# A reordered last slice, finer pieces at its end, a finer start and matmuls on an identity in an attention-over-graphs kernel

## The chip, the cores and the metric

One core of one Trainium2 chip. The metric is the time of one execution on the device in microseconds (us), lowest is best. Engines are named as in the profile: PE or TensorE (matmuls), PEld (its weight loads), DVE or VectorE, ACT or ScalarE, POOL or GpSimd, SP (the queue that issues transfers). "The clock" is the clock that TensorE is granted, as a share of full speed.

## The reference

128 graphs of 128 nodes with 768 features. Each is normalised over its features, cut at zero, projected to queries, keys and values (12 heads of 64), and attends within itself under a mask with an additive bias; the result is added to the input.

```python
def reference(x, adj, Wq, bq, Wk, bk, Wv, bv, beta):
    h = maximum(layernorm(x), 0)                      # x: 128 x 128 x 768, seen as 128 graphs
    q, k, v = heads(h @ Wq + bq), heads(h @ Wk + bk), heads(h @ Wv + bv)     # 12 heads of 64
    s = q @ k.T / 8 + beta * adj
    s = where(adj > 0, s, -9e15)
    return x + merge(softmax(s) @ v)
```

## The kernel before

The graphs go through in 32 groups of four (`GRP = 4`). Per group there are three **slices** of the projection: the queries and keys of six heads ("qk0"), the values ("v") and the queries and keys of the other six ("qk1"). Save for the very first slice, which is computed plainly, each slice is computed in 15 **products** of sums of blocks, with corrections that VectorE adds on. While TensorE works through a slice, the attention of three **head pairs** is fed in between its products: `scores` (16 matmuls in the profile's count, then bias on VectorE and exponential on ScalarE) and, four products later, `attend` (16 matmuls, division on VectorE, addition of the residual on GpSimd, store).

```python
    def bias_1(G, raw):                      # the masked bias of a group, from its adjacency
        a = work.tile([P, GRP, N], F32, tag="adjT", name=f"adjT_{G}", bufs=1)
        nc.vector.transpose(a, raw.rearrange("p g b j -> p g (b j)"))
        kp = work.tile([P, GRP, N], U8, tag="kp", name=f"kp_{G}", bufs=1)
        nc.vector.tensor_scalar(kp, a, 0.0, None, op0=ALU.is_gt)
        nc.vector.tensor_scalar(a, a, beta_c, BIAS_CAP * ISCALE, op0=ALU.mult, op1=ALU.min)
        t = biasT[G] = work.tile([P, GRP, N], F32, tag="biasT", name=f"biasT_{G}", bufs=2)
        nc.gpsimd.memset(t, MASKED)
        nc.vector.copy_predicated(t, kp, a)
        nc.scalar.activation(a, a, AF.Square)
        return a

    def bias_2(G, a):                        # its largest square, for the overflow flag
        bm = stat.tile([P, GRP], F32, tag="bm", name=f"bm_{G}", bufs=1)
        nc.vector.tensor_reduce(bm, a, AX.X, ALU.max)
        nc.vector.tensor_tensor(seen_b, seen_b, bm, ALU.max)
    # ... cut
    def attention(G, u):                     # head pairs 3u, 3u+1, 3u+2, among a slice's products
        todo = {}
        for i in range(3):
            todo.setdefault(1 + 4 * i, []).append(lambda oc=3 * u + i: scores(G, oc))
            todo.setdefault(5 + 4 * i, []).insert(0, lambda oc=3 * u + i: attend(G, oc))
        return todo

    def slice_of(G, sl, todo):
        for n in range(len(PRODUCTS)):
            product(G, sl, n)
            for f in todo.get(n, ()):
                f()
    # ... cut
    HB = GRP * NB // 2
    first = {}

    def half(r, step):                       # the first group is normalised in two halves
        lo = r * HB
        if step == 0:
            for g in range(2):
                stats(0, 2 * r + g)
        elif step == 1:
            first[r] = moments_1(0, lo, lo + HB)
        else:
            first["pool"] = moments_2(0, lo, lo + HB, *first[r])   # ends in a power on GpSimd
            for g in range(2):
                norm(0, 2 * r + g)                                 # ScalarE
            for k in range(3):
                first["dve"] = to_hT(0, r, k)                      # transpositions on VectorE
    # ... cut
    def behind_adds(f, *args):               # puts f behind the latest correction on VectorE
        with tc.issue_after(added[0].ins):
            return f(*args)
    # ... cut: in the loop over the groups, the slice qk1 of group 0
        if not G:
            for n in range(8):
                then(n, lambda n=n: behind_adds(sum_weights, "qk0", n))
            then(13, lambda: bias_2(1, bias_1(1, load_adj(1))))
    # ... cut: after the loop, the last three head pairs, with nothing left to lie beside
    last = attention(NG - 1, 1)
    for n in sorted(last):
        for f in last[n]:
            f()
    # ... cut: worst, over, a matmul and "bad", the overflow flag that decides whether a
    #          second, general program has to run
```

## Time and profile before

| | before |
|---|---|
| time, median of 3 | 3136.41 us (3132.30 to 3136.93) |
| the profiled run | 3132.11 us; span 3130.3 us, mean clock 0.997 |
| TensorE busy | 99% of the span |

The prediction shows the busy line, the list of TensorE's waits, the chain of work at the stall and the tail, and the timeline of the stall. Three more pieces are needed, all from the timeline of the kernel before. Columns: start, length in us, engine and line, operation, written tile <- read tiles, shapes, count, and in brackets the idle time of that engine ahead of it with what ended it.

```profile
10.37 1.66 POOL L244 TENSOR_TENSOR rstd<-ve,nhalf 128x8 f32<-128x8 f32 x1
...
16.68 5.89 PE L402 MATMUL plain<-A,qk_T 128*128 128x256 f32 x16 [6.90 <-DVE A L262]
...
71.52 7.12 ACT L255 ACTIVATE x<-x,shift,rstd 128x192 f32<-128x192 f32 x16 [20.01 <-POOL shift L246]
...
78.55 0.61 ACT L288 ACTIVATE adjT<-adjT 128x512 f32<-128x512 f32 x1
...
79.19 0.69 DVE L293 TENSOR_REDUCE bm<-adjT 128x4 f32<-128x512 f32 x1 [2.85 <-ACT adjT L288]
...
3122.97 1.26 POOL L375 TENSOR_TENSOR xo<-xo,o 128x512 f32<-128x512 f32 x1 [5.50 <-DVE seen L373]
...
3123.14 1.11 DVE L519 TENSOR_SCALAR over<-worst 128x2 f32<-128x2 f32 x1
```

The first two lines are the start: a power on GpSimd ahead of the first normalisations, and the first 16 matmuls, which begin after TensorE has idled for 6.9 us. The next three are a chain across engines: ScalarE normalises group 1 (16 pieces), squares group 0's bias behind them, and VectorE sits 2.85 us waiting for that square. The last two are the end: the comparison for the flag runs at the same time as the last residual addition on GpSimd, and takes 1.11 us for 2 columns.

### The profile page before, as it was taken

How to read it: one execution, taken by the hardware profiler on the slowest of the kernel's cores; microseconds unless marked ns; L12 is line 12 of the kernel's file. 1: busy time of each engine (PE TensorE's matmuls, PEld its weight loads, DVE VectorE, ACT ScalarE, POOL GpSimd, SP SyncE). 2: the span in 40 equal slices, each digit the busy share in tenths (PEclk: the TensorE clock that was granted, in tenths of full speed). 3: DMA queues.
4: the chain of work that ended last, by engine and by line, in shares of the span. 5: the costliest groups of instructions: out<-in, count | busy, mean ns of one | idle time of the engine just before them, and what ended most of it. 6: DMA issues, size and time to landing. Idle time of an engine off the chain costs nothing.

```text
span 3130.3 us, 46295 instructions
## 1 busy us (share of the span) xinstructions
PE 3099.0 (99%) x17822; PEld 2748.1 (88%) x17822; DVE 1999.5 (64%) x5137; ACT 800.6 (26%) x1697; POOL 378.0 (12%) x308
## 2 busy tenths in 40 slices
PE   8999999999999999999999999999999999999998
PEld 7888888888888888888888888888888888888887
DVE  7866566666566665666656666656666566675554
ACT  2222222322222222222222232222222222223221
POOL 1111111111110111111111111111011111111110
PEclk9999999999999999999999999999999999999998
DMA  5212112121122121221211212112211122111111
GB/s 153 70 50 55 43 50 64 51 55 44 45 65 58 48 56 40 57 61 51 55 41 51 65 48 58 44 45 65 57 49 52 44 57 61 51 52 39 49 41 32
DMA packets 358385, 169.94 MB, mean 54 GB/s; under 512 B 84368, under 2 KB 358032, under 8 KB 358160
## 3 DMA queue, kind: packets, MB, share of 16 engines
q1 hardware_dynamic: 355296, 166.14, 19.5%
q8 instruction: 142, 2.33, 0.3%
q10 hardware_dynamic: 2864, 0.79, 0.1%
q14 instruction: 83, 0.68, 0.1%
HBM read 116.53 MB, written 50.33 MB: 53 GB/s over the span
## 4 chain that ended last, share of the span: by engine, by line
PE 98%; DVE 1%; ACT 0%; DMA 0%; issue 0%; POOL 0%; DVEq 0%; ACTq 0%
PE pc_qk L312 18%; PE pb_qk L312 14%; PE pa_qk L312 14%; PE av L364 11%; PE pc_v L312 9%; PE pb_v L312 7%; PE pa_v L312 7%; PE pd_qk L312 7%; PE sc L351 7%; PE pd_v L312 4%; PE plain L402 1%; ACT x L255 0%; DMA x<-in_x_dram 0%; DVE A L262 0%; PE pm L226 0%; PE pm L239 0%
## 5 line engine op out<-in xcount | busy, mean ns | idle before, releaser
L375 POOL TENSOR_TENSOR xo<-xo,o 128x512 f32<-128x512 f32 x192 | 261.1, 1360 | 2455.5 <-DVE seen L373 1539.2
L355 ACT ACTIVATE e<-e 128x512 f32<-128x512 f32 x384 | 235.6, 630 | 780.0 <-DVE e L354 779.3
L364 PEld LDWEIGHTS av<-v,e 128*128 128x128 f32 x3072 | 375.4, 193 | 15.4 <-ACT e L355 5.4
L255 ACT ACTIVATE x<-x,shift,rstd 128x192 f32<-128x192 f32 x512 | 227.9, 533 | 587.4 <-POOL shift L246 587.4
L364 PE MATMUL av<-v,e 128*128 128x65 f32 x3072 | 366.8, 273 | 4.7 <-ACT e L355 4.7
L312 PE MATMUL pb_qk<-S,qk_T 128*128 128x256 f32 x1512 | 367.2, 386 | 0.0
L333 ACT ACTIVATE qk<-pc_qk,bqk 128x256 f32<-128x256 f32 x378 | 158.1, 469 | 726.5 <-PE pc_qk L312 726.5
L354 DVE SCALAR_TENSOR_TENSOR e<-sc,biasT 128x512 f32<-128x512 f32 x384 | 246.8, 685 | 128.2 <-PE sc L351 128.2
L312 PEld LDWEIGHTS pb_qk<-S,qk_T 128*128 128x128 f32 x1512 | 277.3, 190 | 40.2
L337 DVE TENSOR_TENSOR qk<-qk,pb_qk 128x512 f32<-128x512 f32 x252 | 172.1, 683 | 159.4 <-PE pb_qk L312 142.3
L312 PE MATMUL pc_qk<-S,qk_B 128*128 128x256 f32 x1008 | 246.5, 388 | 2.7 <-ACT qk L333 2.7
L312 PE MATMUL pa_qk<-S,qk_T 128*128 128x256 f32 x1008 | 244.7, 386 | 0.0
L312 PE MATMUL pc_qk<-S,qk_T 128*128 128x256 f32 x1008 | 238.1, 379 | 0.0
L351 PE MATMUL sc<-qk 64*128 64x128 f32 x3072 | 224.4, 285 | 0.0
L262 DVE STREAM_TRANSPOSE A<-x 128x256 f32<-128x256 f32 x384 | 217.4, 611 | 8.1 <-ACT x L255 8.0
L312 PEld LDWEIGHTS pc_qk<-S,qk_B 128*128 128x128 f32 x1008 | 187.3, 191 | 33.9 <-ACT qk L333 3.1
L312 PEld LDWEIGHTS pc_qk<-S,qk_T 128*128 128x128 f32 x1008 | 191.5, 190 | 26.0
L351 PEld LDWEIGHTS sc<-qk 64*128 64x128 f32 x3072 | 187.1, 188 | 30.1 <-issue 21.2
L312 PEld LDWEIGHTS pa_qk<-S,qk_T 128*128 128x128 f32 x1008 | 186.3, 190 | 30.4
L312 PE MATMUL pb_v<-v_T,S 128*128 128x256 f32 x768 | 184.2, 382 | 0.0
L337 DVE TENSOR_TENSOR qk<-qk,pd_qk 128x512 f32<-128x512 f32 x126 | 86.6, 688 | 150.0 <-PE pd_qk L312 150.0
L370 DVE TENSOR_TENSOR o<-av,rs 128x256 f32<-128x256 f32 x384 | 160.2, 418 | 2.1 <-DVE seen L373 0.4
(108 smaller groups left out, 4475.1 us busy)
## 6 DMA issues: line engine op xcount, KB each, us to landing
xo<-in_x_dram SPq DMA_DIRECT2D x192, 256.0 KB, 2.8
out_dram<-xo SPq DMA_DIRECT2D x192, 256.0 KB, 2.2
x<-in_x_dram SPq DMA_DIRECT2D x504, 96.0 KB, 2.4
adj<-in_adj_dram SPq DMA_DIRECT2D x128, 64.0 KB, 2.3
qk_T<-in_L_gnn_Wq_dram SPq DMA_DIRECT2D x10, 128.0 KB, 3.4
qk_T<-in_L_gnn_Wk_dram SPq DMA_DIRECT2D x10, 128.0 KB, 3.3
v_T<-in_L_gnn_Wv_dram SPq DMA_DIRECT2D x5, 256.0 KB, 5.5
qk_B<-in_L_gnn_Wq_dram SPq DMA_DIRECT2D x8, 128.0 KB, 3.4
```

The costliest lines, as they stand in the source:

```text
L255: nc.scalar.activation(t, t, AF.Relu, bias=shift[G, n], scale=rstd[G, n])
L262: last = nc.vector.transpose(t[:, :, g * N:(g + 1) * N].rearrange("p c (b i) -> p c b i", i=SQ), src)
L312: nc.tensor.matmul(p[:, i, :], lhs, rhs, start=(first and i == 0 and c == 0), stop=(c == 1), skip_group_check=True)
L333: nc.scalar.activation(t[:, i, :], p[:, i, :], AF.Identity, bias=bqk[:, i, oc:oc + 1], scale=float(sign))
L337: added[G] = nc.vector.tensor_tensor(t, t, p, ALU.add if sign > 0 else ALU.subtract)
L351: nc.tensor.matmul(ps[i][:, g, :], t[r, 1, at], t[r, 0, at], start=True, stop=True)
L354: nc.vector.scalar_tensor_tensor(e, ps[i], SCORE_CAP * ISCALE, biasT[G], op0=ALU.min, op1=ALU.add)
L355: nc.scalar.activation(e, e, AF.Exp, scale=1.0 / ISCALE)
L364: nc.tensor.matmul(pa[:, 2 * g + i, :], es[G, oc, i][:, 2 * r + g, :], vt[G, "v", r, h // 4][:, 4 * g + h % 4, :], start=True, stop=True)
L370: nc.vector.tensor_mul(o[:, r], pa[:, :, 0:HD], rs.to_broadcast([P, 4, HD]))
L375: nc.gpsimd.tensor_add(t, t, o.rearrange("p a (b j) d -> p (a b) (j d)", j=2))
L402: nc.tensor.matmul(p[:, i, :], b[:, c, i * P:(i + 1) * P], a[:, c, :], start=(k == 0 and i == 0 and c == 0), stop=(c == 1), skip_group_che ...
```

## The change

Its intent: (1) the first two graphs are normalised each for itself, so that TensorE's first operand is there earlier; (2) ten matmuls of the identity run in the idle time ahead of it, to bring the clock up; (3) the bias of group 1 is put behind VectorE's corrections in its queue; (4) the last slice's products stand in another order, all six remaining head pairs of the last group are fed in among them, and three of these pairs in halves (two graphs each), with their residual added on VectorE.

```diff
+LAST = (0, 1, 2, 3, 5, 7, 6, 10, 11, 9, 4, 12, 8, 13, 14)
     ... cut: `squares[0]` remembers the second moment matmul; `weigh` is the division taken out of `attend`
+    def scores_half(G, oc, r):               # two graphs: 8 matmuls instead of 16
+        t = xo[G, oc, r] = work.tile([P, 2, P], F32, tag="xo", name=f"xo_{G}_{oc}_{r}", bufs=3)
+        nc.sync.dma_start(t, x[...])
+        ... cut
+    def attend_half(G, oc, r):
+        ... cut
+        weigh(G, oc, r, pa, o)
+        t = xo[G, oc, r]
+        nc.vector.tensor_add(t, t, o.rearrange("p (b j) d -> p b (j d)", j=2))
+        nc.sync.dma_start(out[...], t)
-    def slice_of(G, sl, todo):
-        for n in range(len(PRODUCTS)):
+    def slice_of(G, sl, todo, order=range(len(PRODUCTS))):
+        for at, n in enumerate(order):
             product(G, sl, n)
-            for f in todo.get(n, ()):
+            for f in todo.get(at, ()):
                 f()
-    HB = GRP * NB // 2
+    PARTS = (((0, NB), (NB, 2 * NB)), ((2 * NB, 4 * NB),))
     def half(r, step):
+        for lo, hi in PARTS[r]:
+            ... cut: the same steps, for the graphs of (lo, hi)
+    with tc.issue_after(squares[0].ins):
+        warm = psum.tile([P, P], F32, tag="mm", name="warm")
+        for n in range(10):
+            nc.tensor.matmul(warm, ident, ident, start=True, stop=True)
-            then(13, lambda: bias_2(1, bias_1(1, load_adj(1))))
+            then(13, lambda: bias_2(1, behind_adds(bias_1, 1, load_adj(1))))
-        slice_of(G, "qk1", todo)
-    last = attention(NG - 1, 1)
-    for n in sorted(last):
-        for f in last[n]:
-            f()
+        if G + 1 < NG:
+            slice_of(G, "qk1", todo)
+            continue
+        todo = {}
+        for at, f, *args in (
+            (0, scores, 0), (3, attend, 0), (3, scores, 1), (6, attend, 1), (6, scores, 2), (9, attend, 2),
+            (9, scores_half, 5, 0), (10, scores_half, 4, 0), (11, attend_half, 5, 0), (12, scores_half, 3, 0),
+            (12, attend_half, 4, 0), (13, scores_half, 3, 1), (13, attend_half, 3, 0), (14, scores_half, 5, 1),
+            (14, attend_half, 3, 1), (14, scores_half, 4, 1), (14, attend_half, 5, 1), (14, attend_half, 4, 1),
+        ):
+            then(at, lambda f=f, args=args: f(G, *args))
+        slice_of(G, "qk1", todo, LAST)
```

## The prediction

> **What bounds the kernel now.** I read the page's busy line first, then the list of what the matmul engine waited for over the whole execution, then the chain that ended last in the two places those waits point to.
>
> ```profile
> PE 3099.0 (99%) x17822; PEld 2748.1 (88%) x17822; DVE 1999.5 (64%) x5137; ACT 800.6 (26%) x1697; POOL 378.0 (12%) x308
> ```
>
> ```profile
> PE pm L226 <- DVE st L217: 7.7, 1, 7.7
> PE plain L402 <- DVE A L262: 6.9, 1, 6.9
> PE av L364 <- ACT e L355: 4.7, 3, 1.7
> PE pc_qk L312 <- ACT qk L333: 2.7, 1, 2.7
> PE pf L522 <- DVE over L519: 2.6, 1, 2.6
> PE pm L239 <- DVE dev L233: 0.9, 1, 0.9
> ```
>
> TensorE is busy 3099 of 3130 us, and all its waits are single events: the start (7.7 + 0.9 + 6.9), one stall of 2.7, and the end (4.7 in three pieces, 2.6). So some 3000 us in the middle can't be touched by this change; I compared the built programs' order and from group 1 to the last group's V slice TensorE's stands unchanged. The question is only how many of the microseconds at both edges come back. The chain of work shows what else they cost (start us, length us, what):
>
> ```profile
> 12.81 3.17 ACT x L255 x7
> 16.00 0.64 DVE A L262
> 16.68 5.89 PE plain L402 x16
> ...
> 24.64 26.00 PE plain L402 x120
> ...
> 99.57 3.68 PE pc_qk L312 x8
> 103.25 1.73 PE av L364 x16
> ...
> 3112.43 0.42 PE sc L351 x4
> 3112.85 2.06 PE av L364 x12
> 3114.91 1.63 PE sc L351 x12
> 3116.59 0.70 DVE e L354
> 3117.32 0.64 ACT e L355
> 3118.00 3.69 PE av L364 x16
> ```
>
> Read the same work at two speeds: 120 matmuls of the projection take 26.0 us (217 ns each), the first 16 take 5.89 (368 each); 16 attend matmuls take 1.73 us at 103.25 and 3.69 at 3118.00. After the start, after the stall and in the tail the array runs at half clock. The windows view gives the granted clock: 0.50 from 99.8 to 103.0, and 0.50 from 3113.6 to the end.
>
> **What the Trainium skill says.** (1) "TensorE: Matmul & The Clock Gate", Part 1, "What's actually happening": the array idles at half clock, is released after a busy window of about 3.4 us, and the window runs freely. The trace agrees on the length: the half clock of the stall lasts from 99.6 to 103.0. It differs on the fall: the page asks for an idle window of about 3.4 us, while here 1.67 us of idleness (3110.1 to 3111.77) ahead of 3113.6 was followed by it. The 1.5 us at 3105.2 was not. (2) "SBUF — State Buffer", "SBUF: two separate sides": a VectorE operation in a two-port mode and a GpSimd operation exclude each other for their whole length. The trace fits: VectorE's 128x2 "over" takes 1.11 us, and ends with the GpSimd addition that started at 3122.97 and took 1.26; the 128x1 one beside it takes 0.15.
>
> **Part 1, the first two graphs singly.** Before, the squares' matmul starts at 9.17 and the power on GpSimd at 10.37. It takes 1.66 us for 8 columns and 2.89 for 16 (at 68.07), so 0.154 per column and 0.43 fixed; for 4 columns I estimate 1.04. VectorE's order now has graph 1's mean between graph 0's steps, so graph 0's squares start only about 0.35 earlier. Graph 0: power at 10.0 to 11.05, the scaling of beta (0.3) now behind it, shift done at 11.55, ScalarE at 11.6 instead of 12.35. Graph 1's shift (12.9) comes before graph 0's four normalisations end (13.4), so they run on. The first product starts at 15.9 instead of 16.68: **0.75 us**.
>
> **Part 2, ten identity matmuls.** Twenty instructions behind graph 1's squares. A 128-column pass costs half of 217 warm, so about 0.21 us cold: from 9.8 to 14.1. They hide in idle time. They cover a window, or most of one, and the idle 1.8 us to 15.9 may or may not let the clock fall again. If it stays up, the first 16 cost 3.46 instead of 5.89: **2.4 us**. Against it, the second squares matmul of graphs 2 and 3 now waits for VectorE, which waits for the last query weights (their sums start at 19.6): **0.6 us** lost. Together TensorE is some 2.5 us early by 97 us.
>
> **Part 3, the second group's bias behind the additions** (in the diff, not in its title). At 96.84 TensorE stops because ScalarE's evacuation stands behind two exponentials, and those behind VectorE, which has been full since 79:
>
> ```profile
> 96.85 1.28 DVE L354 SCALAR_TENSOR_TENSOR e<-sc,biasT 128x512 f32<-128x512 f32 x2
> 97.56 1.23 ACT L355 ACTIVATE e<-e 128x512 f32<-128x512 f32 x2 [3.15 <-DVE e L354]
> 98.70 0.82 ACT L333 ACTIVATE qk<-pc_qk,bqk 128x256 f32<-128x256 f32 x2
> 99.57 3.06 PEld L312 LDWEIGHTS pc_qk<-S,qk_B 128*128 128x128 f32 x8 [3.13 <-ACT qk L333]
> ```
>
> From VectorE's queue ahead of 96.85 the change takes the transposition (0.71 start to start), the comparison (0.35), the scaling (0.39) and the masked copy (0.58): 2.0 us. Also, the built order puts group 0's square of the bias after 11 of 16 normalisations instead of 16, and VectorE sat 2.85 us for it; 5 x 0.44 = 2.2 less. So this step comes at 92.6 instead of 96.85 and the product at 95.3 instead of 99.57. TensorE arrives at 94.3, waits 1.0, too little for the clock to fall (1.5 was), and the eight matmuls cost 1.73 instead of 3.68. Gain at this point 4.3 + 1.95 = **6.2 us, all of the head**: the 2.5 of parts 1 and 2 are in it, since the later wait decides. If the clock falls before the first product, 4.8.
>
> **Part 4, the last slice.** Before: its first product starts at 3069.05, the last ends at 3104.1, then scores and attention of three head pairs follow each other with waits and half clock, and the last flag ("bad") is done at 3124.86. After: 15 products x 1.73 = 25.9; three whole scores 3.3 and attends 5.2; four half scores (0.55 each) 2.2 and three half attends (0.87) 2.6; 0.19 after each of five scores, 0.95. The last product ends at T = 3109.2, if nothing waits; each half attend has 3.3 us of other matmuls between it and its scores, against some 1.4 for addition and exponential. Behind T: scores 5 (T+0.65), attend 3 (T+1.5), scores 4 (T+2.1), attend 5 (T+3.0), then the exponential of pair 4, which stands behind attend 3's VectorE work (T+4.0), attend 4 (T+4.7), its division and addition (T+6.0), and worst, over, the flag matmul and bad (T+6.95). That is 3116.2, 8.7 earlier; 0.95 of it is "over", no longer beside a GpSimd addition. I keep 8 for small waits. The added VectorE additions (six of about 0.35) lie beside TensorE save the last.
>
> **Sum.** 6.2 + 8 = 14 us. From the run that was profiled (3132.1) that gives 3118; from the median (3136.4), 3122. The three runs lie at 3132 and 3136.5, as a clock window more or less would put them. I take 3120.
>
> **Rivals.** (a) The clock falls in the 1.8 us before the first product, or isn't released: a third of the phases, by the tail's 1.67. Worth 1.5 to 2, so 3122. (b) VectorE becomes the bound of the last slice: from the ninth product on I count about 18.6 us of its work (six halves of 2.2, eight evacuations of 0.69) in 20 us of TensorE's; if it lags, each half attend waits a little, and if two waits add up within a window the clock falls too: 3 to 5 us lost, 3124. (c) The transfers: only three residual buffers for six halves, and loads and stores in one queue. Counting 2.2 us per store and 2.4 per load, the last half's residual lands 10 us after the first half's store at T-6.6, so at T+3.4, some 2 us before it is wanted. Near, but hidden; if it isn't, 1 to 2 us. (d) Part 3 only moves VectorE's backlog, and a later evacuation stalls instead: the scores after next have 4.6 us in hand before, so I think not.
>
> **Range and chances.** The steps add to 14 with some 4 either way, and the start's phase adds 2: 3114 to 3127. Both edges together are under 2% of 3136 (63 us), so a change of 2% is out of reach unless something breaks: faster 0.01, within 0.985, slower 0.005.
>
> **What would show it.** Right: the first product at about 15.9 with 16 matmuls in 3.5; no stall over 1.5 at 93 to 97 and no half clock there; first product of the last slice to the flag 47 us instead of 55.8; "over" at 0.15. Wrong: half clock after the start; attend waiting for exponentials before the last product; VectorE waiting for a residual load; a new stall between 100 and 120.

## The result, and the profile after

| | before | after |
|---|---|---|
| time, median of 6, alternating on one chip | 3134.36 us (3131.43 to 3136.93) | 3119.93 us (3118.41 to 3120.09) |
| the profiled run | 3132.11 us | 3119.99 us |
| span, mean clock | 3130.3 us, 0.997 | 3118.2 us, 0.999 |

The ratio is 0.9953 (0.9940 to 0.9966): the same within 2%, and 14.7 us less. Ratios here are the mean time of one kernel's fast runs over that of the other's of the same rounds, so not quite the ratio of the medians.

A word on the kernel before, whose times lie in two clusters: of its 27 timings beside the experiments 18 lie near 3132 and nine at 3135.7 to 3138.8. The records show a mean clock of 0.997 for the first and 0.995 or 0.994 for the second. The clusters therefore go with the clock; where in the execution it was lost is not shown, because no execution of the upper cluster was profiled. The changed kernel keeps within 3118.1 to 3120.1 (the six above and the five of e12 below). So the two profiled runs, 12.1 us apart, compare the lower cluster with the changed kernel, and the 14.7 of the means has the upper cluster in it.

The busy line of the changed kernel's page, and the head of its list of TensorE's waits over the whole execution (line, what released it: us in total, times, longest):

```profile
PE 3099.8 (99%) x17846; PEld 2748.6 (88%) x17846; DVE 2000.8 (64%) x5155; ACT 801.1 (26%) x1703; POOL 375.8 (12%) x307
```

```profile
PE pm L228 <- DVE st L219: 7.2, 2, 5.8
...
PE plain L443 <- DVE A L266: 1.6, 1, 1.6
PE pc_qk L316 <- ACT qk L337: 1.2, 1, 1.2
...
PE av L411 <- ACT e L403: 0.2, 1, 0.2
```

The stall in the middle has shrunk from 2.7 to 1.2, and the waits of the attend matmuls in the tail from 4.7 to 0.2. The 6.9 ahead of the first product is 1.6 because the identity matmuls now fill that time; that is no gain by itself.

**The start and the stall.** From the chain of the changed kernel that ended last (start, length, what):

```profile
16.11 5.13 PE plain L443 x16
...
96.78 1.99 PE pc_qk L316 x8
98.77 1.73 PE av L379 x16
```

The attend matmuls behind the stall start at 98.77 instead of 103.25, which is **4.48 us** earlier. The first product of the last slice starts at 3064.57 instead of 3069.05, again 4.48: nothing is gained or lost in the 3000 us between. The eight matmuls behind the stall take 1.99 instead of 3.68, so the clock no longer falls there. But the first 16 take 5.13, where at full clock they take 3.72 (e5 below); by an estimate, 2.8 of the 5.13 us are at half clock, twice the 1.41 lost. That is read from the durations. The clock column of the windows view is no witness for the start: for this profile it shows 1.00 from 9 to 21 us.

The timeline of the changed kernel, for the lines that correspond to those shown of before:

```profile
10.14 1.02 POOL L248 TENSOR_TENSOR rstd<-ve,nhalf 128x4 f32<-128x4 f32 x1 [7.53 <-DVE ve L246]
...
72.39 4.93 ACT L259 ACTIVATE x<-x,shift,rstd 128x192 f32<-128x192 f32 x11 [22.20 <-POOL shift L250]
...
77.87 0.69 DVE L297 TENSOR_REDUCE bm<-adjT 128x4 f32<-128x512 f32 x1 [2.78 <-ACT adjT L292]
...
94.05 1.28 DVE L358 SCALAR_TENSOR_TENSOR e<-sc,biasT 128x512 f32<-128x512 f32 x2
...
96.78 1.99 PE L316 MATMUL pc_qk<-S,qk_B 128*128 128x256 f32 x8 [1.20 <-ACT qk L337]
...
3109.71 0.88 PE L411 MATMUL av<-v,e 128*128 128x65 f32 x6 [0.23 <-ACT e L403]
...
3112.03 0.17 DVE L576 TENSOR_SCALAR over<-worst 128x2 f32<-128x2 f32 x1
...
3112.67 0.14 DVE L582 CAST bad<-nbad 1x1 int32<-1x1 f32 x1
```

The power for four columns takes 1.02 us. The square of the bias now stands behind 11 normalisations and not 16, yet VectorE still waits 2.78 us for it: the normalisations begin at 72.39 where they began at 71.52, although TensorE was 1.33 us earlier.

**The tail.** From the first product of the last slice to the end of the flag it is 3112.81 - 3064.57 = 48.24 us; it was 3124.86 - 3069.05 = 55.81. That is **7.57 us** less. "over" takes 0.17 instead of 1.11. Behind the flag 5.39 us remain, before 5.44. The two gains and this 0.05 make up the 12.1 us between the spans.

### The profile page after: what moved, and what is told of

It is laid out like the page before. It is cut to its first block, busy times and chain, and to the rows that moved or that the text cites. A ratio compares the mean times of both kernels' runs of the same rounds, so it can differ in the third digit from the quotient of the medians.

```text
span 3118.2 us, 46382 instructions
## 1 busy us (share of the span) xinstructions
PE 3099.8 (99%) x17846; PEld 2748.6 (88%) x17846; DVE 2000.8 (64%) x5155; ACT 801.1 (26%) x1703; POOL 375.8 (12%) x307
## 3 DMA queue, kind: packets, MB, share of 16 engines
q1 hardware_dynamic: 355392, 166.14, 19.4%
## 4 chain that ended last, share of the span: by engine, by line
PE 98%; DVE 1%; DMA 0%; ACT 0%; issue 0%; SPq 0%; ACTq 0%; DVEq 0%
PE pc_qk L316 18%; PE pb_qk L316 14%; PE pa_qk L316 14%; PE av L379 10%; PE pc_v L316 9%; PE pb_v L316 7%; PE pa_v L316 7%; PE pd_qk L316 7%; PE sc L355 7%; PE pd_v L316 4%; PE plain L443 1%; DMA x<-in_x_dram 0%; ACT x L259 0%; DVE A L266 0%; PE av L411 0%; PE pm L228 0%
## 5 line engine op out<-in xcount | busy, mean ns | idle before, releaser
L379 PEld LDWEIGHTS av<-v,e 128*128 128x128 f32 x3024 | 367.4, 192 | 9.8
L379 PE MATMUL av<-v,e 128*128 128x65 f32 x3024 | 358.2, 272 | 0.0
```

The costliest lines, as they stand in the source:

```text
L379: nc.tensor.matmul(pa[:, 2 * g + i, :], es[G, oc, i][:, 2 * r + g, :], vt[G, "v", r, h // 4][:, 4 * g + h % 4, :], start=True, stop=True)
```

## The experiments

The theory to test was the prediction's: part 3 removes most of the stall, the start's gain is hidden behind it, and the tail gains from attention in halves among the products. Twelve runs, the last of them the changed kernel again, were made on three chips, each beside nine runs of the kernel before on the same chip. The 95% intervals of the ratios are some 4 us wide on either side, with both clusters among the nine; differences of medians compare with the lower cluster, and effects of one or two us rest on the profiles.

### The parts alone (median of before 3132.37 of 9)

**e1_tail_only**: the kernel before with part 4.

```diff
-    PARTS = ...                       (of the changed kernel: parts 1 to 3 undone)
-    with tc.issue_after(squares[0].ins): ...
-            then(13, lambda: bias_2(1, behind_adds(bias_1, 1, load_adj(1))))
+            then(13, lambda: bias_2(1, bias_1(1, load_adj(1))))
```

> The kernel before with the last slice's new order and half attention alone. Theory (the gain is the sum of two separate edges): from the last slice's first product to the flag 48.2 us as in the changed kernel instead of 55.8, everything up to 3069 as before, half clock from 99.6 to 103.0 still there; the time 7 to 8.5 us under the kernel before. Rival (the head carries most, and the tail merely keeps its clock because the head shifted it): under 4 us, and half clock again in the last slice.

3125.13 us (3123.72 to 3128.77), ratio 0.9975 (0.9961 to 0.9988). By the medians the tail alone brings 7.2 us, and from the last slice's first product to the flag it is 48.24 us, as in the changed kernel. The stall is as in the kernel before: a wait of 2.7, and the eight matmuls behind it at half clock. As expected.

**e2_bias_only**: the kernel before with part 3.

```diff
-            then(13, lambda: bias_2(1, bias_1(1, load_adj(1))))
+            then(13, lambda: bias_2(1, behind_adds(bias_1, 1, load_adj(1))))
```

> The kernel before with the second group's bias held behind the additions, nothing else. Theory (VectorE's queue decides the stall): the second pair's scores 2.0 us earlier on VectorE than 96.85, so the stalled product starts at about 97.5 instead of 99.57, TensorE idle about 0.7, no half clock after it, the next attend at 99.3 instead of 103.25: about 4 us faster. Rival (the stall comes from the start of the kernel, and the bias only fills idle time): the product within 0.5 us of 99.57 and half clock after it, under 1 us faster.

3129.36 us (3129.07 to 3130.05), ratio 0.9988 (0.9974 to 1.0002), so 3.0 us by the medians; the interval just holds 1. The timeline at the stall:

```profile
98.56 1.99 PE L312 MATMUL pc_qk<-S,qk_B 128*128 128x256 f32 x8 [1.24 <-ACT qk L333]
```

The wait falls from 2.7 to 1.24, the matmuls behind it take 1.99, and no half clock follows. So the theory holds, but for less than it foretold: the product came 1.0 us earlier and not 2, in part because the first 16 took 6.41 here and 5.89 in the profile of before. This one line, which isn't in the change's title, is the larger share of what the head gained.

**e3_start_only**: parts 1 and 2, with the old bias and the old tail.

```diff
-            then(13, lambda: bias_2(1, behind_adds(bias_1, 1, load_adj(1))))      (of the changed kernel)
+            then(13, lambda: bias_2(1, bias_1(1, load_adj(1))))
+    last = attention(NG - 1, 1)       (and the loop over it, as before)
```

> The changed kernel with the old bias placement and the old tail: single normalisation and identity matmuls alone. Theory (the later wait decides): TensorE 1.3 us early by the first group's projection, but the second pair's scores still behind the bias on VectorE, so the product after the stall at 98.5 to 99.2, TensorE idle about 3 us, half clock after it; 0.5 to 1.2 us faster than before. Rival (the steps add, the start carries the head): 2.5 us or more faster.

3131.08 us (3130.59 to 3132.57), ratio 0.9994 (0.9981 to 1.0008): 1.3 by the medians, little above what the theory allowed; the interval holds 1. But the profile speaks against the theory's reason:

```profile
97.89 3.46 PE L316 MATMUL pc_qk<-S,qk_B 128*128 128x256 f32 x8 [2.50 <-ACT qk L337]
```

The stall's matmuls begin at 97.89 instead of 99.57: the start's gain is not hidden behind the stall, it moves the stall. The wait stays at 2.50.

**e4_no_warm**: the changed kernel without part 2.

```diff
-    with tc.issue_after(squares[0].ins):
-        warm = psum.tile([P, P], F32, tag="mm", name="warm")
-        for n in range(10):
-            nc.tensor.matmul(warm, ident, ident, start=True, stop=True)
```

> The changed kernel without the ten identity matmuls. Theory (in the profiled run they ended without releasing the clock, so they gave little of their own): the first product at 16.1 again, the first 16 matmuls in 5 to 6 us, according to where the clock window lies; the built order puts the first group's square after 15 instead of 11 normalisations, so the product after the stall comes up to 1.8 us later than 96.78; 0 to 1.8 us slower than the changed kernel, so 13 to 14.6 faster than before. Rival (they release the clock, and 2.4 us of the head hang on it): 2.4 us or more slower than the changed kernel.

3120.49 us (3119.60 to 3120.59), ratio 0.9958. Its first 16 take 6.36, 1.23 more than in the changed kernel, and it is some 0.5 us slower by the median, 0.7 at the stalled product of the profiles. So ten identity matmuls bring about half a microsecond, too little for the medians to prove. (The 13 to 14.6 under before that were expected came out as 11.9, and in e7 below the 14 to 14.6 as 12.7: these ranges seem to be set from the 14.4 to 14.7 of the result, which has the upper cluster in it.)

By the medians the parts alone sum to 7.2 + 3.0 + 1.3 = 11.5 us; the changed kernel, timed on another chip as e12 below, is 12.8 under before there. As far as medians tell, they are nearly additive, where the prediction had the start inside the stall.

### Why the identity matmuls did not bring the clock up (median of before 3132.66 of 9)

Two explanations: multiplying an identity, mostly zeros, isn't counted as work; or ten are too few.

**e5_warm14_ident** and **e6_warm14_data**, one look each:

```diff
-        for n in range(10):
-            nc.tensor.matmul(warm, ident, ident, start=True, stop=True)
+        for n in range(14):
+            nc.tensor.matmul(warm, ident, ident, start=True, stop=True)       # e5
+        some = xg[0, 3][:, 0, 0:P]
+            nc.tensor.matmul(warm, some, some, start=True, stop=True)         # e6
```

> The changed kernel with fourteen identity matmuls instead of ten. Theory (the clock is released by a sufficiently busy window, whatever the operands; ten end too early for the window of the profiled run): 28 passes at half clock last 6.2 us, from 9.8 to 16.0, and hold nearly a whole window of 3.4 us; passes fall from 0.21 to 0.11 us within them, and the first 16 projection matmuls take 3.5 to 4.2 us instead of 5.1. Rival (multiplying the identity isn't counted as work): all 28 passes at half clock, the first product delayed to about 16.3, and its first 16 matmuls at 5 us or more.

> The same with fourteen matmuls of a piece of the input by itself instead of the identity (their result is used by nobody). Theory (any operands count): as with the identity, first 16 projection matmuls 3.5 to 4.2 us. Rival (the identity isn't counted): passes fall to 0.11 us here but not with the identity, and the first 16 take 3.5 to 4.2 us only here.

3118.85 and 3118.75 us, one run each. The timeline of e5:

```profile
9.86 6.14 PE L491 MATMUL warm<-ident 128*128 128x128 f32 x28
...
16.13 3.72 PE L443 MATMUL plain<-A,qk_T 128*128 128x256 f32 x16
```

With fourteen the first 16 take 3.72, at full clock from the start; with data in place of the identity they take 3.72 too. In e5 the 28 passes themselves stayed at half clock (6.14), as the rival had it, and in e6 they did not (5.13); but that is not the operand, since in e11 below 28 identity passes took 4.87. So an identity counts as work, and ten were too few to be sure. How often ten suffice the seven profiles with ten show: the first 16 took 3.72 once (e8 below), and 5.12 to 5.41 in the six others. These six are of two kinds. In three (after, e3, e9) all twenty passes took 4.61 us together, so the clock came up neither during them nor soon after. In the other three (e7, e10, e12) the passes took 3.99 to 4.18, so it came up during them, and after 2.1 to 2.3 us of idleness it fell again. The windows view of e12 shows it (columns: stretch, length, busy time and instructions of PE, PEld, DVE, ACT, POOL, then the clock, the share of the transfer engines, GB/s):

```profile
15.00:16.00 1.00, 0.34 (x2) 0.31 (x3) 1.00 (x2) 0.00 (x0) 0.00 (x0) 1.00 0.83 212
16.00:17.00 1.00, 1.00 (x4) 0.82 (x3) 1.00 (x4) 0.00 (x0) 0.00 (x0) 0.51 0.85 244
...
19.00:20.00 1.00, 1.00 (x5) 0.86 (x4) 0.30 (x1) 0.00 (x0) 0.00 (x0) 0.79 1.14 256
```

The clock is granted in full up to 16.0, 0.35 us into the first product, and at half to 19.4: the clock falls, as rival (a) of the prediction has it. The Trainium skill, "TensorE: Matmul & The Clock Gate", Part 1, "What's actually happening", has a free-running window of about 3.4 us that must be busy for the release. TensorE's early stretch in the changed kernel, from 8.98 to 14.46, holds one whole such window in a part of the phases only; an estimate from that figure is that a stretch is certain to hold one from 6.8 us on, and e5's, from about 9.0 to 16.0, is that long. A stretch of 5.5 us would hold one in 2.1 of 3.4, some 60% of the phases, by the same estimate; with ten, the clock came up in four of the seven (e7, e8, e10, e12). The runs agree with it. A window is not seen in them as such.

### What the tail's gain rests on

**e7_old_order_halves**: the old order of the products, with the halves where that order has their inputs ready. **e8_new_order_whole**: the new order, with the last three pairs whole.

```diff
-            (9, scores_half, 5, 0), (10, scores_half, 4, 0), ... (14, attend_half, 4, 1),
+            (9, scores_half, 3, 1), (11, scores_half, 5, 0), (11, attend_half, 3, 1), ...   # e7
-        slice_of(G, "qk1", todo, LAST)
+        slice_of(G, "qk1", todo)                                                            # e7
+            (13, scores, 3), (14, scores, 5), (14, attend, 3), (14, scores, 4),             # e8
+            (14, attend, 5), (14, attend, 4),
```

> The changed kernel with the last slice's products in their old order, and the half attention put at the places where that order completes its blocks. Theory (cutting the attention in halves and putting it among the products is what pays, the order of products hardly): both orders leave the same five half pieces behind the last product, so first product to flag 48 to 48.8 us, and the time within 0.7 us of the changed kernel (14 to 14.6 faster than before). Rival (the new order is needed, so that blocks are complete in time): matmuls wait in the second half of the slice, 50 us or more, 2 us or more slower than the changed kernel.

> The changed kernel with the new order of products but whole attention for the last three head pairs, as early as their blocks allow (one pair's scores before the last product). Theory (halves pay mostly by what they leave behind the last product): behind it 7.4 us of matmuls instead of 3.9, a longer last division, and VectorE's over again beside a GpSimd addition (1.1 us): first product to flag 50 to 51.5, 2 to 3 us slower than the changed kernel. Rival (the order is what pays): within 0.7 us of the changed kernel.

e7: 3119.95 us (3118.71 to 3120.11), ratio 0.9954. First product of the slice to the flag: 48.23 us, as in the changed kernel (48.24). **With halves, the order of the products is worth nothing here**, as expected.

e8: 3118.62 us (3117.97 to 3119.59), ratio 0.9951. **Here the theory fell.** It expected 50 to 51.5 us from first product to flag for whole pairs, and measured were 3110.99 - 3062.98 = 48.01. The last lines of e8's timeline:

```profile
3103.53 3.80 PE L379 MATMUL av<-v,e 128*128 128x65 f32 x32
...
3109.10 1.26 POOL L383 TENSOR_TENSOR xo<-xo,o 128x512 f32<-128x512 f32 x1 [0.95 <-DVE o L367]
...
3109.34 1.04 DVE L574 TENSOR_SCALAR over<-worst 128x2 f32<-128x2 f32 x1
```

32 attend matmuls run without a wait: a whole pair's scores and another pair's attend are long enough to cover the addition and exponential of the pair between. TensorE is done 3107.33 - 3062.98 = 44.35 us after the slice's first product; with halves it is 46.04. The halves cost 1.7 us of TensorE's time: 0.2 is a wait, and the rest goes with more frequent switches between kinds of matmul (eight of scores took 0.65, and eight of attend 0.84 once and 1.03 to 1.05 three times; the prediction had 0.55 and 0.87). They give it back behind TensorE, 2.20 us to the flag against 3.66: a half is divided in half the time, and "over" is not beside a GpSimd addition. So neither the halves nor the new order is needed for the tail's 7.57: each can be left out alone. (Both left out at once was not run; by e7's list the third pair is complete at the same place in the old order, so there is no sign against it.) What e1, e7 and e8 have in common is that the last three pairs' scores and attends are staggered, each exponential beside the matmuls of another pair; before, each pair's attend waited for the exponential just issued. The timelines fit that in size. The waits fall from 4.7 to 0.2, which is 4.5. The half clock behind them, from 3113.6 on, goes too: there 12 attends took 2.06, 12 scores 1.63 and 16 attends 3.69, and at the rates of full clock (1.73 for 16 attends, 1.09 for 16 scores) they would take 1.30, 0.82 and 1.73, which is 3.5. "Over" gives 0.9, and the switches take some 1.5 back. That is 7.4 of 7.57.

### The rest of the stall, and a better version (median of before 3132.78 of 9)

**e9_max_later**: the changed kernel, with group 0's maximum of the squares, for which VectorE waited 2.8 us, moved behind the second pair's scores.

```diff
-                then(10, lambda: bias_2(0, behind_adds(bias_1, 0, adj_0)))
+                then(10, lambda: squared.append(behind_adds(bias_1, 0, adj_0)))
+            then(7, lambda: behind_adds(bias_2, 0, squared[0]))     # in the slice qk1 of group 0
```

> The changed kernel with the first group's maximum of squared biases (0.69 us on VectorE, which waits 2.8 us for ScalarE's square ahead of it) moved behind the second pair's scores. Theory (the remaining 1.2 us stall hangs on VectorE's queue, and that on the wait for the square): that wait gone, the second pair's scores come 1.5 us or more earlier relative to TensorE's work, and TensorE no longer stops at 97; 1.2 us faster than the changed kernel for the same start. Rival (the queue only shifts, because it is held by TensorE's and ScalarE's pace): the stall stays within 0.4 us of 1.2.

3118.18 us (3117.03 to 3119.97), ratio 0.9949 (0.9935 to 0.9963); the changed kernel itself, run again beside it as e12, has 3119.95. The timeline of e9, at the place of the stall:

```profile
95.15 1.89 PE L316 MATMUL pc_qk<-S,qk_B 128*128 128x256 f32 x8
```

No bracket, so no wait: the stall is gone, and 1.8 us with it by the medians (1.2 by the stall alone). The maximum and VectorE's wait for the square ahead of it were what remained; the edit moves both, so the 0.69 us of the maximum itself are not set apart from the wait.

**e10_add_last**: e8, with the last residual addition on VectorE, behind the flag.

```diff
+        with tc.issue_after(flag.ins):            # flag: the copy into "bad"
+            store(nc.vector, NG - 1, 4, left[0])  # left out of attend(NG - 1, 4), on GpSimd in e8
```

> The variant with whole attention in the new order, whose VectorE over took 1.04 us beside a GpSimd addition, with that last addition done on VectorE behind the flag instead. Theory (the two exclude each other): over takes 0.15 to 0.2 us, first product to flag 47.1 instead of 48.0. Rival (over is slow because of its tiny shape or its waits): over stays near 1 us and the flag at 48.0.

3118.53 us (3117.98 to 3120.61). The timeline's last instructions:

```profile
3111.19 0.17 DVE L582 TENSOR_SCALAR over<-worst 128x2 f32<-128x2 f32 x1
...
3112.03 0.69 DVE L391 TENSOR_TENSOR xo<-xo,o 128x512 f32<-128x512 f32 x1
```

"over" takes 0.17 with no GpSimd addition beside it and 1.04 with one (e8): the same operation on the same tiles. First product to flag is 47.13, 0.88 less than in e8, as expected. But the span ends 6.84 us after the flag instead of 5.51, because the addition and its store now come last. Most of the gain is given back; against e8, timed on another chip, the medians show nothing. The path to the flag has a second operation of this kind, which e10 and e11 leave in: the 4-column maximum `seen` with two inputs takes 0.63 us beside the last GpSimd addition that is left, and ends with it (in e10 at 3110.00 and 3109.99), where elsewhere it takes 0.13.

**e11_all**: e10, with fourteen identity matmuls and e9's move. **e12_changed_again**: the changed kernel on the same chip.

```diff
-        for n in range(10):
+        for n in range(14):                       # e11: and the diffs of e9 and e10
```

> All that paid together: whole attention in the new order with the last addition behind the flag, fourteen identity matmuls, the maximum moved back. If the gains add: first product to flag 47.1, first 16 projection matmuls 3.7 us, no stall at 97; about 3 us faster than the changed kernel, 3116 to 3117. If they don't (the later wait absorbs the start): 1 us faster at most.

> The changed kernel unaltered, for comparison on the same chip as the three before it and for another position of the clock window: 3118 to 3120.5; first 16 projection matmuls 3.5 us if the clock was released before 16, 5 us or more if not, and the product after the stall at 95.3 or 96.8 accordingly; stall 1.2 us in either case.

e11: 3117.26 us (3116.86 to 3117.53), ratio to before 0.9945 (0.9932 to 0.9959). Its first product to the flag is 47.12, as foretold. e12: 3119.95 (3118.08 to 3120.00), ratio 0.9951; its first 16 took 5.41, its stalled product stands at 96.59 and its stall is 1.2, within what was expected. So e11 is the best version, 2.7 us under the changed kernel and 15.5 under before on that chip. It also spreads least: its first 16 take 3.72, and it has no stall.

## Why the prediction was right or wrong

The time was right, 3120 foretold and 3119.93 measured, but the close hit is luck. The sum, 6.2 + 8 = 14, was too large by two: against the lower cluster the changed kernel gains 4.5 + 7.6 = 12.1. The middle between 3132 and 3136 as the starting point made up for it. Every part gained, the identity matmuls least, and no new stall came; what failed are part 3's "the later wait decides" and the reason given in part 4.

**Part 1, 0.75.** Right: 0.57 (16.68 to 16.11), and in the ten other profiles with it the first product came at 15.66 to 16.13, against 16.63 to 17.03 in the three without (before, e1, e2). The power for four columns, estimated at 1.04, took 1.02.

**Part 2, 2.4 at the first 16, less 0.6.** Wrong in size: "if it stays up, the first 16 cost 3.46" did not come about. They cost 5.13, 0.76 less than in the profile of before and about 1.2 less than in e1, e2 and e4 (6.30 to 6.41), which have no identity matmuls either. The rival given a third of the phases happened in six of seven profiles with ten matmuls. The 0.6 set against it, for a wait of the second squares matmul, did not appear either.

**Part 3, 6.2 for the whole head, "since the later wait decides".** This is the step that failed. It took VectorE's queue for a clock of its own, so that the start could be early or late without moving the stall. The profiles say otherwise (end of the first 16 and start of the stalled product, from the chains; wait from the list of waits; e6, e7, e10 and e12, left out, lie at 75.51 to 75.53 with 1.2, and e11, which has e9's move, at 74.36 with none):

| | end of first 16 | stalled product | between | wait |
|---|---|---|---|---|
| before | 22.57 | 99.57 | 77.00 | 2.7 |
| e1 (old bias) | 23.33 | 100.34 | 77.01 | 2.7 |
| e3 (old bias, new start) | 21.06 | 97.89 | 76.83 | 2.5 |
| e2 (new bias, old start) | 23.04 | 98.56 | 75.52 | 1.2 |
| after | 21.24 | 96.78 | 75.54 | 1.2 |
| e4 (no identity matmuls) | 22.24 | 97.48 | 75.24 | 1.0 |
| e5 (fourteen) | 19.85 | 95.41 | 75.56 | 1.2 |
| e8 (clock up) | 19.65 | 95.19 | 75.54 | 1.2 |
| e9 (maximum later) | 20.98 | 95.32 | 74.34 | none |

The distance is fixed by the order of the work and not by the start: with the new bias four starts (e2, after, e5, e8), spread over 3.4 us, all leave 75.5, and e4, with another order on ScalarE, 75.2. So VectorE's queue hangs on TensorE. Two links stand in the traces: VectorE's corrections wait for TensorE's products (in the changed kernel 2.65 us at 51.09, 0.44 at 52.81 and 57.99), and group 1's second moment matmul stands among TensorE's products, with the power, the normalisations, the square and VectorE's wait for the square behind it. Which of them carries the distance was not separated; only the end of the second was cut. Without that wait and the maximum behind it (e9) the distance shrinks by 1.2, the whole remaining stall. The head's 4.48 is then 1.33 of an earlier start (22.57 to 21.24), passed on in full; 1.46 of a shorter distance, from part 3; and 1.69 of the matmuls behind the stall at full clock (3.68 to 1.99, foretold as 1.95).

Within part 3, the term "5 x 0.44 = 2.2 less" measured 0.07: VectorE's wait was 2.78 instead of 2.85. The five normalisations fewer were real, but the moment matmul had moved back by as much. It starts 67.67 - 21.24 = 46.43 us after the first 16 in the changed kernel, and 66.84 - 22.57 = 44.27 before (starts from the chains); the square stands at 55.99 and 55.98. The statistics that it needs end on VectorE 43.13 us after the first 16 in the changed kernel (63.24 + 1.13) and 40.27 before (61.71 + 1.13), and the matmul itself then waits 0.20 us for VectorE. I had read the new order on ScalarE and not the ones on VectorE and TensorE that feed it. The stall of 1.0 foretold came out at 1.2 because TensorE, too, came later than foretold.

**Part 4, 8.7, kept 8.** Measured 7.57. The last product ended 41.0 us after the slice's first (40.15 foretold), and the flag 7.2 behind that (6.95). Missing are chiefly the switches: half scores at 0.65 and half attends mostly at 1.03 to 1.05. The wait before the end was small (0.23), and rivals (b) and (c), VectorE as the bound and the residual transfers, did not show. Right in size, then, but e8 shows that the halves aren't what pays.

**"Over", 0.95.** Right: 1.11 to 0.17, and e10 shows it apart from the rest. The prediction's comparison with "the 128x1 one beside it" was no test: that one ran at 2941.13, with nothing on GpSimd at the time. That the operation is in a two-port mode no run shows.

**Open.** Where the kernel before loses its clock in the upper cluster. And why e9 gains 1.8 by the medians for a stall of 1.2: its runs vary by 2.9 us, so 0.6 may be scatter. And the tail with old order and whole pairs together, which was not run.

## What to carry to other kernels

Before saying that a later wait hides an earlier gain, follow the waiting engine's queue back to what feeds it: if that is the engine that waits, the gain passes through in full, and the same distance between two events in kernels with different starts shows it. At the end of a kernel stagger the pieces so that each has another's matmuls to hide its exponential; cutting them finer costs switches, and moving work behind the flag only pays if its store doesn't become the end. Matmuls that are to raise the clock must be enough and must end close to the first real one: here fourteen, which left 0 to 1.4 us idle, did it in three of three, and ten, which left 1.6 to 2.3, in one of seven.

## What the Trainium skill lacked or had wrong

- "TensorE: Matmul & The Clock Gate", Part 1, "What's actually happening": the half clock is put down to an idle window of about 3.4 us (a later section of the page has it come and go with frequent short idling, without a length). Here it fell after windows that were partly busy: in e12 at 16.0, with TensorE idle for 2.3 us of the window before, and in the tail of before at 3113.6, with 1.83 of the 3.4 us busy. The length of the half clock, 3.4 us (16.0 to 19.4), agrees.
- The same page: it says that a release takes one busy window, that the window runs freely and that the moment of release varies with it, but not how long a warm-up must be to be sure of it. Ten identity matmuls (4.0 to 4.6 us) gave the first product full clock in one of seven profiles, fourteen (4.9 to 6.1 us) in three of three.
- The same page doesn't say whether matmuls on mostly zero data count as activity. They do: 3.72 us for the first 16 with an identity and with data.
- "SBUF — State Buffer", "SBUF: two separate sides": that the loser is blocked for the other's whole instruction is stated; a figure for a tiny operation isn't. Two columns on VectorE took 1.04 us beside a GpSimd addition, to whose end it waited, and 0.17 without it.
- No page read for this case gives the time of a power on GpSimd: 1.02 us for 4 columns, 1.66 for 8, 2.90 for 16 (by the spans of the profile, which are rough on GpSimd).
- "TensorEngine Tiling (Array Packing)", "Key Properties", says that a change of tiling mode drains TensorE, without a cost. The scores here are 64*128 and the other matmuls 128*128: the eight of a product take 1.92 us behind scores and 1.73 behind another product, and the same three pairs in halves kept TensorE 1.7 us longer than whole (0.2 of it a wait).
